# First stage of a four-layer graph network on one core: the order of x, the adjacency masks and the slice-logit fold

## Chip, core and metric

The kernel runs on one core of a Trainium2 chip. The metric is the device time of one execution in microseconds (us): the median of 3 runs was 2817.94 us (2809.52 to 2823.55). The execution that the profiler recorded took 2806.95 us, of which 2805.2 us lie between its first and its last instruction (the span).

## The reference, cut to what matters

The network has four layers on 2708 nodes with 256 features. Each layer adds a graph step over a dense 2708x2708 adjacency matrix (int32) and then a feed-forward step. The change touches the graph step of layer 0 and one small product of its feed-forward step:

```python
# graph step, features = layernorm(x)
Qn, Kn = cos_normalize(features @ Wq.T), cos_normalize(features @ Wk.T)   # 128 columns each
att = softmax(where(adj > 0, Kn @ Qn.T, NEG), axis=1)
prop = where(sum(adj, 1) > 0, att @ features, features)
x = x + 0.5 * prop + 0.5 * features
# feed-forward step, its slice weights
xm = (layernorm(x) @ W_x.T + b_x) per head                                # 8 heads of 64
sw = softmax((xm @ W_slice.T + b_slice) / max(temperature, 1e-6))
```

## The kernel before, in words

Nodes are cut into 22 tiles of 128 rows (NT = 22, the last has 20). The first stage, `cosine_gnn`, has two parts.

**Projection.** x (tile X, line 180) is read in three pieces and a rest: tiles 0 to 7 on SP's DMA queue, 8 to 15 on ACT's, 16 to 20 on SP's. `ln_stats` computes mean and variance of each tile on DVE (lines 144 and 145), their roots on ACT (147) and reciprocals on DVE (151). Then the 22 tiles go by 12 groups, ten pairs and two single tiles: `project` writes the normalised features F (DVE, line 108), transposes them on PE (tp, 225), copies them on ACT (ft, 227) and multiplies them by the weights wqk (pq, 123); `normalise` squares and sums on ACT (sq, 239), takes roots (nrm, 241 to 243), scales (qk, 245, DVE), transposes (pt, 251, PE) and copies to QK (254, half on DVE and half on ACT).

**Score blocks.** The 2708 target nodes are cut into 6 blocks, five of 512 columns and one of 148. For each block and each of the 22 tiles j: a score matmul into PSUM (273; three buffers named score), exp on ACT (275), multiplication by the mask on DVE (281), and up to four matmuls into the accumulators acc (284). In fp32 each of these matmuls stands as two instructions in the profile. After a block, DVE and ACT copy the accumulators and update X (293 to 301).

**Masks.** `columns(i0, iw)` fetches one block of the transposed adjacency in 8 pieces of up to 128x3x512 int32 (raw, 768 KB, line 194, SP's queue, four buffers) and turns each into bytes of the resident mask tile on DVE (198). Before, `columns` of the first two blocks stands ahead of the projection, and that of block n+2 at the head of block n. The whole rows of the adjacency (row, 1354 KB each, line 204, SP's queue, three buffers) are summed on ACT (`degree`, 210), one tile after every fourth exp.

**Fold.** `slice_logits` multiplies W_x by W_slice and the temperature ahead of everything, so that the slice step later needs one matrix wf and one bias bf (lines 326 to 363): 32 matmul instructions wfp (348), 16 bfp (357), 2 bfb (362), some small DVE work (343 to 360) and a copy on ACT (363). Its weights wx, bx, ws, bs and ti come over POOL's queue, and so does wqk. The mask tile occupies memory that the fold's tiles leave, so the memset of its last tile (165, POOL) and all conversions follow the fold.

**Order.** A scheduler in the tile framework puts each engine's instructions into one fixed order when the kernel is built; each engine then runs its list in that order. `issue_after(i)` makes the scheduler put what stands under it behind instruction i. SP's DMA queue is also a list in order: a request that waits for a free buffer holds all requests behind it. After the blocks, SP writes the mask to memory (kept, 303), and `clear_dispatch` writes 8 zero pieces of 2838 KB each (hs, 2235); before, the scheduler mixes these with the rows. The next stage, `slice_ffn`, runs over the 22 tiles with pl (wf), the slice softmax on DVE and ACT, and z; its weights outw, outb, wfx, hyin, hyout come over POOL's queue.

Of the kernel before, what the change touches and what calls it, by code (L numbers as in the profile page):

```python
# [8 lines left out]
F32 = mybir.dt.float32  # L9
# [3 lines left out]
ALU = mybir.AluOpType  # L13
# [3 lines left out]
P = 128  # L17
N = 2708
D = 256
# [16 lines left out]
def rows(t):  # L36
    return min(P, N - t * P)


def span(t):  # L40
    return slice(t * P, t * P + rows(t))


def chunks(width):

    return [(c, min(width, N - c)) for c in range(0, N, width)]
# [108 lines left out]
        return inverse_root(self.net, pool, self.mv[:, t0:t1, 1], 1.0, LN_EPS, "nr", self.rstd[:, t0:t1])  # L155


def cosine_gnn(net, ctx, kept, x_in):

# [4 lines left out]
    with ExitStack() as ctx:  # L166
        big = ctx.enter_context(tc.tile_pool(name="g0big", bufs=1))
        rawp = ctx.enter_context(tc.tile_pool(name="g0raw", bufs=4))
        rowp = ctx.enter_context(tc.tile_pool(name="g0row", bufs=3))
        F = big.tile([P, NT, D + 1], F32, name="F")  # L170
        QK = big.tile([P, 2, N], F32, name="QK")
        den = big.tile([P, NT], F32, name="den")
# [1 line left out]
        total = big.tile([P, NT], F32, name="total")  # L174

        nrm = big.tile([P, NT, 2], F32, name="nrm")
        w = net.load_weight(big, a["wqkT"], "wqk")
        full = N // P * P
        for t0, t1, engine in ((0, 8, nc.sync), (8, 16, nc.scalar), (16, NT - 1, nc.sync)):
            engine.dma_start(X[:, t0:t1, :], x_in[t0 * P : t1 * P].rearrange("(t p) d -> p t d", p=P))  # L180
        nc.scalar.dma_start(X[: N - full, NT - 1, :], x_in[full:])
        nc.gpsimd.memset(F[:, :, D : D + 1], 1.0)
# [3 lines left out]
        GR = 3  # L186
        groups = [range(t, min(t + GR, NT - 1)) for t in range(0, NT - 1, GR)] + [range(NT - 1, NT)]

        def columns(i0, iw):

            for g in groups:
                t0, n, r = g[0], len(g), rows(g[0])
                raw = rawp.tile([P, GR, 512], I32, name="raw")
                nc.sync.dma_start(
                    raw[:r, :n, :iw],
                    a["adjT"][t0 * P : t0 * P + (n - 1) * P + r, i0 : i0 + iw].rearrange("(t p) i -> p t i", p=r),
                )
                nc.vector.tensor_scalar(
                    net.mask[:r, t0 : t0 + n, i0 : i0 + iw], raw[:r, :n, :iw], 0.0, None, ALU.is_gt
                )  # L200

# [7 lines left out]
            r = rows(i)  # L209
            nc.scalar.activation(row[:r], row[:r], AF.Copy, accum_out=total[:r, i : i + 1])  # L210

        columns(*chunks(512)[0])
        columns(*chunks(512)[1])
        ln = net.ln_stats()
        with tc.tile_pool(name="g0p", bufs=2, space=PSUM) as psum, tc.tile_pool(name="g0w", bufs=3) as work:
            pairs = [range(t, t + 2) for t in range(0, NT - 2, 2)] + [range(NT - 2, NT - 1), range(NT - 1, NT)]
# [16 lines left out]
            def normalise(g):  # L233
                n, r, t0 = len(g), rows(g[0]), g[0]
                pq = held.pop(g)
                sq = work.tile([P, P], F32, name="sq")
                for k, t in enumerate(g):
                    for m in range(2):
                        nc.scalar.activation(sq[:r], pq[:r, k, m], AF.Square, accum_out=nrm[:r, t, m : m + 1])
                v = nrm[:r, t0 : t0 + n, :]  # L240
                nc.scalar.activation(v, v, AF.Sqrt)
                nc.vector.tensor_scalar(v, v, 1e-4, None, ALU.max)
                nc.vector.reciprocal(v, v)
                qk = work.tile([P, 2, 2, P], F32, name="qk")
                nc.vector.tensor_tensor(
                    qk[:r, :n], pq[:r, :n], v.unsqueeze(3).to_broadcast([r, n, 2, P]), ALU.mult
                )
                pt = psum.tile([P, 2, 2, P], F32, name="pt")
                for k in range(n):
                    for m in range(2):  # L250
                        nc.tensor.transpose(pt[:, m, k, :r], qk[:r, k, m], net.ident[:r, :r])
                nodes = slice(t0 * P, t0 * P + (n - 1) * P + r)
                for m, engine in ((0, nc.vector.tensor_copy), (1, nc.scalar.copy)):
                    engine(QK[:, m, nodes], pt[:, m].rearrange("p k b -> p (k b)")[:, : (n - 1) * P + r])

            for n, g in enumerate(pairs):
                project(g)
                if n:
                    normalise(pairs[n - 1])
            normalise(pairs[-1])  # L260
        work = ctx.enter_context(tc.tile_pool(name="g0work", bufs=3))
        psc = ctx.enter_context(tc.tile_pool(name="g0s", bufs=3, space=PSUM))
        pacc = ctx.enter_context(tc.tile_pool(name="g0a", bufs=1, space=PSUM))
        for n, (i0, iw) in enumerate(chunks(512)):
            its = tiles_of(i0, iw)
            adj_rows = {i: load_rows_of(i) for i in its}
            if n + 2 < len(chunks(512)):
                columns(*chunks(512)[n + 2])
            acc = [pacc.tile([P, D + 1], F32, name=f"acc{k}", tag=f"acc{k}") for k in range(len(its))]
            for j in range(NT):  # L270
                r = rows(j)
                ps = psc.tile([P, 512], F32, name="score")
                nc.tensor.matmul(ps[:r, :iw], QK[:, 0, span(j)], QK[:, 1, i0 : i0 + iw], start=True, stop=True)  # L273
                e = work.tile([P, 512], F32, name="e")
                exp = nc.scalar.activation(e[:r, :iw], ps[:r, :iw], AF.Exp)  # L275

                if j % 4 == 1 and 0 <= j // 4 - 1 < len(its):
                    i = its[j // 4 - 1]
                    with tc.issue_after(exp.ins):
                        degree(i, adj_rows[i])  # L280
                nc.vector.tensor_tensor(e[:r, :iw], e[:r, :iw], net.mask[:r, j, i0 : i0 + iw], ALU.mult)  # L281
                for k, i in enumerate(its):
                    ri = rows(i)
                    nc.tensor.matmul(  # L284
                        acc[k][:ri], e[:r, k * P : k * P + ri], F[:r, j, :], start=j == 0, stop=j == NT - 1
                    )
            nc.vector.tensor_scalar(
                deg[:, its[0] : its[-1] + 1], total[:, its[0] : its[-1] + 1], 0.0, None, ALU.is_gt
            )
# [10 lines left out]
                nc.vector.scalar_tensor_tensor(X[:r, i, :], g[:r, :D], s[:r, 0:1], X[:r, i, :], ALU.mult, ALU.add)  # L300
                nc.vector.scalar_tensor_tensor(X[:r, i, :], F[:r, i, :D], s[:r, 1:2], X[:r, i, :], ALU.mult, ALU.add)
        for t in range(NT):
            nc.sync.dma_start(kept[span(t), :], net.mask[: rows(t), t, :])
        nc.vector.tensor_scalar(net.empty, den, 0.0, None, ALU.is_equal)


def inverse_root(net, pool, v, scale, eps, name, out=None):
# [15 lines left out]
    return y if out is None else last  # L323


def slice_logits(net, pool):


    nc, tc, a = net.nc, net.tc, net.a
    H, G, HC = 8, 64, 512  # L330
    wf = pool.tile([P, 2, HC], F32, name="wf")
    bf = pool.tile([P, HC], F32, name="bf")
    with tc.tile_pool(name="s_f", bufs=1) as fp, tc.tile_pool(name="s_fp", bufs=1, space=PSUM) as psum:
        wx = fp.tile([64, H, D], F32, name="wx")
        nc.gpsimd.dma_start(wx, a["w_x"].rearrange("(h p) c -> p h c", p=64))
        bx = fp.tile([64, H], F32, name="bx")
        nc.gpsimd.dma_start(bx, a["b_xT"])
        ws = fp.tile([64, G], F32, name="ws")
        nc.gpsimd.dma_start(ws, a["w_sliceT"])
        bs = fp.tile([1, G], F32, name="bs")  # L340
        nc.gpsimd.dma_start(bs, a["b_slice"].partition_broadcast(1))
        ti = net.load_rows(fp, a["temperature"], H, "ti")
        nc.vector.tensor_scalar(ti, ti, 1e-6, None, ALU.max)
        nc.vector.reciprocal(ti, ti)
        for c in range(2):
            ps = psum.tile([P, H, G], F32, name=f"wfp{c}")
            for h in range(H):
                nc.tensor.matmul(ps[:, h, :], wx[:, h, c * P : (c + 1) * P], ws, start=True, stop=True)
            nc.vector.tensor_tensor(
                wf[:, c, :].rearrange("p (h g) -> p h g", g=G),  # L350
                ps,
                ti.unsqueeze(2).to_broadcast([P, H, G]),
                ALU.mult,
            )
        pb = psum.tile([1, H, G], F32, name="bfp")
        for h in range(H):
            nc.tensor.matmul(pb[:, h, :], bx[:, h : h + 1], ws, start=True, stop=True)
        b0 = fp.tile([1, H, G], F32, name="b0")
        nc.vector.tensor_tensor(b0, pb, bs.unsqueeze(1).to_broadcast([1, H, G]), ALU.add)
        nc.vector.tensor_tensor(b0, b0, ti[0:1].unsqueeze(2).to_broadcast([1, H, G]), ALU.mult)  # L360
        pbb = psum.tile([P, HC], F32, name="bfb")
        nc.tensor.matmul(pbb, net.ones[0:1, :], b0.rearrange("p h g -> p (h g)"), start=True, stop=True)
        nc.scalar.copy(bf, pbb)
    return wf, bf


def slice_ffn(net, wf, bf, early):
# [1839 lines left out]
def net_kernel(ctx, tc, a, out):  # L2207
# [4 lines left out]
    net.hs = dram.tile([Routing.E * CAP, D + 2], F32, name="hs")  # L2212
    with ExitStack() as graph:
        with ExitStack() as early:
            folded = slice_logits(net, early.enter_context(tc.tile_pool(name="s_wf", bufs=1, side="right")))
            cosine_gnn(net, graph, kept, a["x"])
            clear_dispatch(net, net.const)
            slice_ffn(net, *folded, early)
        with ExitStack() as mixture:
            biased_gnn(net, *top1_ffn(net, mixture))  # L2220
    with ExitStack() as mixture:
# [129 lines left out]
```

## Time and profile before

| what | value |
|---|---|
| median of 3 runs | 2817.94 us |
| profiled execution, span | 2806.95 us, 2805.2 us |
| busy share of the span: PE, DVE, ACT, POOL | 93%, 52%, 37%, 13% |
| mean granted TensorE clock | 0.965 |
| 0 to 77.5 us, up to the first score | PE busy 44.88 us, DVE 59.97 us |
| 77.5 to 407 us, the score blocks | PE busy 325.82 of 329.50 us |
| 407 us to the end, not touched by the diff but for its start | 2398.2 us |

The profile is read in views: busy time of each engine in stretches of the span, groups of instructions by line, who waited for whom, the chain of work that ended last (each step is followed back to what released it), and a timeline of single instructions. Times in these views count from the first instruction. A busy PE is one with matmuls in its pipe, not one at its peak rate.

### The profile page before, as it was taken

What the parts mean: (1) busy time and instruction counts of PE and PEld (TensorE: products, weight loads), DVE (VectorE), ACT (ScalarE), POOL (GpSimd) and SP (SyncE); (2) the same over time, 40 slices, a digit from 0 to 9 for tenths busy, and PEclk for the clock granted to TensorE, in tenths of its full rate; (3) what the DMA queues carried; (4) which work ended last, traced back from release to release, by engine and by line L of the source; (5) the groups of instructions that cost most, each with busy time, mean ns of one, the idle gap of its engine ahead of it and who ended that gap; (6) DMA issues with size and microseconds to landing.
All of it is one profiled execution on the core that took longest, in us unless ns stands there. A gap on an engine that the chain in (4) does not pass through costs nothing.

```text
span 2805.2 us, 32369 instructions
## 1 busy us (share of the span) xinstructions
PE 2603.2 (93%) x11710; PEld 1611.2 (57%) x11710; DVE 1454.0 (52%) x3102; ACT 1040.9 (37%) x1641; POOL 377.2 (13%) x470
## 2 busy tenths in 40 slices
PE   5999999798999999969799989999989999969998
PEld 4667746574333444558588743333346777757885
DVE  7753348543777776332554456554664222255555
ACT  3444443314565662321444322233332222234453
POOL 1000012100000001134130013323331111110002
PEclk9999999787999999989899999999999999989999
DMA  8899420000000002654310010000121111040001
GB/s 294 287 290 304 149 69 1 3 5 1 1 1 1 1 1 85 173 168 133 108 33 1 1 36 23 18 1 24 77 99 64 35 33 33 25 168 33 1 1 40
DMA packets 106874, 197.70 MB, mean 70 GB/s; under 512 B 8846, under 2 KB 63736, under 8 KB 103876
## 3 DMA queue, kind: packets, MB, share of 16 engines
q1 hardware_dynamic: 88010, 146.82, 16.9%
q0 software_dynamic: 14896, 43.89, 4.8%
q10 hardware_dynamic: 3806, 4.85, 0.6%
q8 instruction: 99, 1.62, 0.2%
q14 instruction: 63, 0.52, 0.1%
HBM read 135.82 MB, written 59.71 MB: 70 GB/s over the span
## 4 chain that ended last, share of the span: by engine, by line
PE 77%; DVE 8%; issue 5%; DMA 4%; ACT 3%; POOL 2%; SPq 0%; ACTq 0%; POOLq 0%; DVEq 0%
PE acc L1311 15%; PE acc L805 8%; PE acc L284 7%; PE h L2031 7%; PE den L816 4%; PE po L2063 4%; PE po L1872 4%; PE score L273 3%; PE sc L1852 3%; PE pv L123 3%; PE h L943 2%; PE sc L1818 2%; PE po L123 2%; DMA dys<-y,to 2%; PE pl L123 1%
## 5 line engine op out<-in xcount | busy, mean ns | idle before, releaser
L675 DVE SCALAR_TENSOR_TENSOR e<-e,mask 128x768 f32<-128x768 f32 (+2 forms) x264 | 412.1, 1576 | 304.4 <-ACT e L674 304.3
L674 ACT ACTIVATE e<-big_p,minus_one,ratio 128x768 f32<-128x768 f32 (+2 forms) x264 | 394.8, 1513 | 367.0 <-PE acc L1311 229.8
L1311 PE MATMUL acc<-V,e 128*128 128x257 f32 (+1 forms) x1936 | 433.5, 383 | 4.5 <-DVE e L675 4.4
L1311 PEld LDWEIGHTS acc<-V,e 128*128 128x128 f32 (+1 forms) x1936 | 352.3, 186 | 85.7 <-issue 32.1
L805 PE MATMUL acc<-e,V 128*64 128x512 f32 (+1 forms) x1056 | 242.7, 548 | 4.4 <-DVE e L675 4.4
L2031 PE MATMUL h<-w,ft 128*128 (+1 forms) x752 | 234.1, 453 | 0.5 <-DVE dso_far L1497 0.5
L284 PE MATMUL acc<-F,e 128*128 128x257 f32 x968 | 226.3, 384 | 3.0 <-DVE e L281 2.6
L284 PEld LDWEIGHTS acc<-F,e 128*128 128x128 f32 x968 | 173.4, 185 | 66.9 <-DVE e L281 28.4
L805 PEld LDWEIGHTS acc<-e,V 128*64 128x64 f32 x1056 | 107.9, 137 | 161.8 <-issue 129.2
L1852 PE MATMUL sc<-qt,kt 64*128 64x512 f32 (+5 forms) x568 | 170.1, 566 | 4.1 <-ACT e L1866 2.4
L2048 DVE TENSOR_TENSOR hh<-hh,h 128x682 f32<-128x682 f32 x47 | 40.7, 865 | 247.5 <-PE h L2031 247.5
L2031 PEld LDWEIGHTS h<-w,ft 128*128 128x128 f32 x752 | 135.9, 191 | 56.5 <-issue 1.8
L1866 ACT ACTIVATE e<-sc 128x1024 f32<-128x1024 f32 (+4 forms) x121 | 100.2, 857 | 183.1 <-PE sc L1852 167.8
L281 DVE TENSOR_TENSOR e<-e,mask 128x512 f32<-128x512 f32 (+2 forms) x132 | 80.4, 625 | 149.0 <-ACT e L275 147.3
L1878 DVE TENSOR_TENSOR sum<-sum,e 128x1024 f32<-128x1024 f32 (+5 forms) x95 | 104.7, 1102 | 74.5 <-ACT e L1866 71.2
L2063 PE MATMUL po<-w,ht 114*128 (+1 forms) x564 | 131.6, 383 | 5.3 <-DVE ht L2056 5.3
L275 ACT ACTIVATE e<-score 128x512 f32<-128x512 f32 (+2 forms) x132 | 69.7, 544 | 179.0 <-PE score L273 152.1
L1872 PE MATMUL po<-e,V 128*64 128x512 f32 (+4 forms) x484 | 112.3, 542 | 17.5 <-DVE e L1870 9.0
L816 PE MATMUL den<-e,low 128*3 128x512 f32 (+1 forms) x1056 | 123.8, 542 | 0.3 <-DVE e L675 0.3
L2063 PEld LDWEIGHTS po<-w,ht 114*128 114x128 f32 x564 | 107.5, 191 | 27.8 <-DVE ht L2056 12.9
L273 PE MATMUL score<-QK 128*128 128x512 f32 (+2 forms) x264 | 112.1, 554 | 1.2 <-ACT e L275 0.7
L1852 PEld LDWEIGHTS sc<-qt,kt 64*128 64x128 f32 (+1 forms) x568 | 58.4, 188 | 89.3 <-issue 74.0
(639 smaller groups left out, 3463.3 us busy)
## 6 DMA issues: line engine op xcount, KB each, us to landing
row<-in_adj SPq DMA_DIRECT2D x21, 1354.0 KB
raw<-in_adjT SPq DMA_DIRECT2D x35, 768.0 KB
hs<-zero SPq DMA_DIRECT2D x8, 2838.0 KB
hidden<-hr SPq DMA_DIRECT2D x32, 256.0 KB
wd<-in_f_wd SPq DMA_DIRECT2D x8, 1024.0 KB
kept<-mask SPq DMA_DIRECT2D x21, 338.5 KB
mask<-kept SPq DMA_DIRECT2D x21, 338.5 KB
w<-in_d_w1T SPq DMA_DIRECT2D x8, 682.0 KB
```

The costliest lines, as they stand in the source:

```text
L123: self.nc.tensor.matmul(out, lhsT[:, c, :], rhs[:, c, :], start=first and c == 0, stop=last and c == n - 1)
L273: nc.tensor.matmul(ps[:r, :iw], QK[:, 0, span(j)], QK[:, 1, i0 : i0 + iw], start=True, stop=True)
L284: nc.tensor.matmul(acc[k][:ri], e[:r, k * P : k * P + ri], F[:r, j, :], start=j == 0, stop=j == NT - 1)
L674: nc.scalar.activation(v, big_p[:, i], AF.Relu, bias=net.minus_one, scale=ratio)
L675: return nc.vector.scalar_tensor_tensor(v, v, 1.0, net.mask[:, j, i], ALU.add, ALU.mult)
L805: made = nc.tensor.matmul(acc[n][half, :iw], V[:, j, h, :], e[:, k, i0 : i0 + iw], start=j == 0, stop=j == NT - 1)
L816: made = nc.tensor.matmul(den[g : g + Q, :iw], low[:, j, h, Q - 1 - q : 2 * Q - 1 - q], e[:, k, i0 : i0 + iw], start=False, stop=j == NT - ...
L1311: nc.tensor.matmul(acc[k][:ri], e[:, k * P : k * P + ri], V[:, j, :], start=j == 0, stop=j == NT - 1)
L1852: nc.tensor.matmul(by_pairs(ps[:r, g])[:, :, o:], kt[b, span(j)], qt[b, :, o:iw], start=True, stop=True)
L1872: nc.tensor.matmul(by_pairs(po[b])[:, :, o:], V[:r, j, g, :], by_pairs(e[:r, g])[:, :, o:], start=j == 0, stop=j == last,)
L2031: last = nc.tensor.matmul(halves[s, n][:, q, :HALF], fts[s][:, c, :], weights.w13[n][:, es[s], c, q * HALF : (q + 1) * HALF], start=c == 0 ...
L2063: last = nc.tensor.matmul(po, ht[:KP, k, :], w2[:KP, es[s], k, :], start=k == 0, stop=k == KC - 1)
```

## The change

- x comes in four pieces and a rest; wx moves from POOL's queue to SP's, behind x; wqk from POOL's queue to the head of ACT's.
- `columns` becomes a generator. The conversions of block 0 (`own`) are put one behind the normalisation of each of two late pairs, and then one behind the masked product of every third tile of block 0. Those of block n+1 (`ahead`) are put behind the masked product of tiles 1, 4, 7, ... 19 and 21 of block n.
- The rows have two buffers, not three. `degree` stands behind the exps of tiles 9, 12, 15 and 18. The rows of block 0 are asked for at its tile 9 behind the pieces asked for by then.
- The fold's matmuls stand between the score blocks, one step behind each of blocks 1 to 4, and take a score buffer in PSUM; its weights stay in the stage's pool.
- `clear_dispatch` is put behind the last kept store.

```diff
-        w = net.load_weight(big, a["wqkT"], "wqk")
+        w = net.load_weight(big, a["wqkT"], "wqk", nc.scalar)
-        for t0, t1, engine in ((0, 8, nc.sync), (8, 16, nc.scalar), (16, NT - 1, nc.sync)):
+        for t0, t1, engine in ((0, 4, nc.sync), (4, 8, nc.sync), (8, 16, nc.scalar), (16, NT - 1, nc.sync)):
...
-        rowp = ctx.enter_context(tc.tile_pool(name="g0row", bufs=3))
+        rowp = ctx.enter_context(tc.tile_pool(name="g0row", bufs=2))
...
-                nc.vector.tensor_scalar(
+                yield nc.vector.tensor_scalar(
                     net.mask[:r, t0 : t0 + n, i0 : i0 + iw], raw[:r, :n, :iw], 0.0, None, ALU.is_gt
                 )
...
-        columns(*chunks(512)[0])
-        columns(*chunks(512)[1])
+        own = columns(*chunks(512)[0])
+        folded.load(big)
...
                 if n:
-                    normalise(pairs[n - 1])
+                    done = normalise(pairs[n - 1])
+                    if len(pairs) - n in (2, 4):
+                        with tc.issue_after(done.ins):
+                            next(own)
...
+        fold = folded.fold(psc, "score")
         for n, (i0, iw) in enumerate(chunks(512)):
             its = tiles_of(i0, iw)
-            adj_rows = {i: load_rows_of(i) for i in its}
-            if n + 2 < len(chunks(512)):
-                columns(*chunks(512)[n + 2])
+            ahead = columns(*chunks(512)[n + 1]) if n + 1 < len(chunks(512)) else iter(())
+            if n:
+                adj_rows = {i: load_rows_of(i) for i in its}
...
-                if j % 4 == 1 and 0 <= j // 4 - 1 < len(its):
-                    i = its[j // 4 - 1]
+                if n == 0 and j == 9:
+                    with tc.issue_after(raws[-1].ins):
+                        adj_rows = {i: load_rows_of(i) for i in its}
+                if j % 3 == 0 and 0 <= j // 3 - 3 < len(its):
+                    i = its[j // 3 - 3]
                     with tc.issue_after(exp.ins):
                         degree(i, adj_rows[i])
-                nc.vector.tensor_tensor(e[:r, :iw], e[:r, :iw], net.mask[:r, j, i0 : i0 + iw], ALU.mult)
+                masked = nc.vector.tensor_tensor(e[:r, :iw], e[:r, :iw], net.mask[:r, j, i0 : i0 + iw], ALU.mult)
+                with tc.issue_after(masked.ins):
+                    if j % GR == 0 and n == 0:
+                        next(own, None)
+                    if j % GR == 1 or j == NT - 1:
+                        next(ahead, None)
...
+            if 0 < n < 5:
+                with tc.issue_after(last.ins):
+                    next(fold)
...
-            folded = slice_logits(net, early.enter_context(tc.tile_pool(name="s_wf", bufs=1, side="right")))
-            cosine_gnn(net, graph, kept, a["x"])
-            clear_dispatch(net, net.const)
-            slice_ffn(net, *folded, early)
+            folded = SliceLogits(net, early.enter_context(tc.tile_pool(name="s_wf", bufs=1, side="right")))
+            stored = cosine_gnn(net, graph, kept, a["x"], folded)
+            with tc.issue_after(stored.ins):
+                clear_dispatch(net, net.const)
+            slice_ffn(net, folded.wf, folded.bf, early)
```

The new `SliceLogits.fold` holds the old statements in four steps: the bias product bfp with its two DVE operations; bfb with the copy bf; the first half of wf; the second half. Each step takes one buffer of the score pool.

## Prediction

> **What bounds the kernel now.** I read four views. First the chain of work that ended last, cut to the first 560 us: before the first score it is not PE's work.
>
> ```profile
> 0.82 11.73 DMA X<-in_x
> ...
> 27.31 2.08 PE bfb L362 x2
> 29.42 6.73 DVE mask L198 x4
> 36.15 1.62 DVE F L108 x5
> ...
> 77.49 6.25 PE score L273 x10
> ```
>
> See the order: x (12.55 us), the fold's end (29.4), mask conversions, and the first score only at 77.49. Second, the waits of the first 130 us and the groups of instructions there:
>
> ```profile
> POOL mask L165 <- PE bfb L362: 23.6, 1, 23.6
> L198 DVE TENSOR_SCALAR mask<-raw 128x1536 uint8<-128x1536 int32 (+1 forms) x34 | 53.1, 1587 | 6.9 <-DMA raw<-in_adjT 6.0 <-PE bfb L362 0.9
> L348 PE MATMUL wfp<-ws,wx 64*128 64x64 f32 x32 | 7.1, 419 | 12.5 <-DMA ws<-in_w_sliceT 12.5
> L357 PE MATMUL bfp<-ws,bx 64*1 64x64 f32 x16 | 1.9, 308 | 0.0
> L362 PE MATMUL bfb<-b,ones 1*128 1x512 f32 x2 | 2.1, 1136 | 6.0 <-DVE b L360 6.0
> ```
>
> The mask's memory is held by the fold for 23.6 us, and 53.1 us of conversions follow on DVE. Third, busy time by stretch (us, then busy us of PE, PEld, DVE, ACT, POOL, granted clock, DMA share, GB/s):
>
> ```profile
> 30.10:77.50 47.40, 33.96 (x177) 26.46 (x177) 42.91 (x76) 26.47 (x125) 1.70 (x1) 1.00 0.79 265
> 77.50:140.90 63.40, 62.16 (x225) 42.32 (x226) 45.44 (x54) 25.15 (x35) 0.00 (x0) 0.97 0.85 298
> 140.90:201.00 60.10, 58.67 (x222) 40.96 (x222) 30.55 (x78) 26.19 (x36) 0.00 (x0) 1.00 0.98 286
> 201.00:259.40 58.40, 58.34 (x222) 40.97 (x221) 22.14 (x63) 25.91 (x36) 0.00 (x0) 1.00 1.07 309
> ```
>
> During the projection DVE is busy 42.91 of 47.40 us: it is the bound. In block 2, without conversions, PE is busy 58.34 of 58.40 us: it is the bound, and what stands on PE there costs its full length. Blocks 0 and 1, which share DVE with conversions, lose only 1.2 and 1.4 us of PE. Fourth, the timeline shows how close a group of three tiles runs in a block:
>
> ```profile
> 105.64 2.74 PE L273 MATMUL score<-QK 128*128 128x512 f32 x6
> 107.33 0.69 DVE L281 TENSOR_TENSOR e<-e,mask 128x512 f32<-128x512 f32 x1 [0.85 <-ACT e L275]
> 108.22 5.37 PE L284 MATMUL acc<-F,e 128*128 128x257 f32 x24
> ```
>
> With the scores from S, the first masked product ends at S+2.38 and its accumulation starts at S+2.58: no slack.
>
> **The change part by part.** I read the order in which the changed kernel's instructions stand on each engine, and put durations of the rows on it.
>
> *1. x and the fold ahead of the projection.* DVE's list has eleven tile statistics (tiles 0 to 10) before the first F, so the piece X[8:16] gates it. Ahead of its end on ACT's queue stand wqk and itself, 1.31 MB; with as much sent for SP that is 2.6 MB. Before, 2.50 MB had moved by 11.25 us (222 GB/s); 0.77 MB by 5 us (154 GB/s) and then the 334 GB/s of 5 to 7.5 us would give 2.6 MB at 10.5 us. I take 11. Tile 8's statistic stood at 16.08, so DVE's list moves up by 5.1 us, and the fold's operations leave it (2.7 us by starts): the last F of the first twelve ends at 28.55 - 7.8 = 20.8 us. PE no longer waits for bfb: its first transposes can run at 14 instead of 30.15. Roots on ACT (the fifth at 17.5), four squares at 0.40 and two ft copies at 0.47, then nrm and qk put the first pt near 23.0, against 39.21.
>
> [...]
>
> *2. Projection without conversions.* From the first pt to the last were 37.5 us for 11 groups, 3.41 each, with a 1.66 us conversion between most. Without: pt to the DVE half of QK 0.69, 0.46 to the ACT half, 0.27 for it, and nrm through qk to the next pt 1.49 (57.15 to 58.64), 2.9 us. PE's own work is 2.8, ACT's 2.55. Eight such, 23.2; the short last groups as before less a conversion, 2.4 + 1.5 + 1.6 + 0.75 = 6.3; the two conversions left, half hidden, 1.7. First score: 23.0 + 23.2 + 6.3 + 1.7 = 54.2 us, so **-23.3 us**. Bounds: 3.41 kept, 61.3 us, -16; ACT alone the limit, about 50, -27.
>
> *3. Conversions beside the scores.* Six conversions of block 0 itself and, in each block, 8 of the next one move under PE's bound. Where the list has product, conversion, product inside a group of three, the second product starts at S+3.96 and its accumulation at S+4.85, while PE is done with the first at S+4.31: 0.5 us. So stand six groups of block 0 (3.0, where 1.3 was idle before: +1.7) and three groups of blocks 1, 2 and 3 (+4.5); block 4 converts narrow pieces within the slack. Bounds: nothing, as blocks 0 and 1 lost little; or the whole 1.66 in all 15 groups, 25 us. I take 0.5, worked from the group's own starts. At the block ends PE's list now has five scores (4.3 us) while DVE finishes X in 3.6: the 1.4 us stall behind block 0 goes, -1.4.
>
> *4. DMA.* A raw buffer is asked for when its conversion four places earlier is done: 16 us ahead in block 0, 31 us later. Block 0 needs 14 MB, 220 GB/s over 63 us, blocks 1 to 3 190; 298 and 309 were moved. Rows with two buffers are asked for 6 tiles, 16 us, ahead, and a waiting row holds the raws behind it. I cost this at nothing; the cover is the 16 us against 10.1 us, the longest landing in the chain (104.62). hs, 22.7 MB, moves behind kept, by my estimate (300 GB/s) 350 to 430 us, beside POOL's weights; outb then lands a few us later, while PE has three tiles of f in hand; hs is not used before 1731 us. Nothing.
>
> *5. degree on the last exp of a group.* Before, two groups a block ran 5.47 instead of 5.20 us. -0.5 x 5 = -2.5 us; bounds 0 and -2.7.
>
> *6. Fold on PE.* It leaves a stretch that part 1 has counted and comes onto the bound: 32 wfp at 0.13 (a warm pt's pitch; 0.22 as they ran at 12.49), 16 bfp at 0.06 to 0.12, bfb 2 x 0.43 (1.04 as it ran): 4.2 + 1.4 + 0.9 = **+6.5**, bounds 5.6 and 11. Its DVE work (0.67 each) still fits under five scores.
>
> *7. Start of the slice stage.* Its list now has the first tile's softmax before the second tile's tp and pl, so three pl (1.73 each) follow instead of filling. The softmax itself ends 2.3 us sooner without its neighbour's operations; the second pt comes near 17.6 instead of 16.0 us after the first tp: +1.6, bounds 0 and 4.
>
> **Sum:** -23.3 + 1.7 + 4.5 - 1.4 - 2.5 + 6.5 + 1.6 = **-12.9 us**. Against the profiled execution, 2806.95 - 12.9 = 2794 us (span about 2792). The median of the runs shown is 11 us above that execution, so I put the same difference on it: 2817.94 - 12.9 = 2805 us.
>
> **Rivals.**
> A. *The blocks cover everything.* Blocks 0 and 1 speak for it: conversions there cost PE almost nothing. Then conversions cost 0 and the idle 1.3 goes, the fold is 5.6, the slice start 0: -23.3 - 1.3 - 1.4 - 2.5 + 5.6 = -22.9, 2795 us. Against it: those conversions were placed freely, these are pinned.
> B. *The start gains little.* ACT (26.47 us busy of 47.40) and the pq-to-pt loop keep 3.41 us a group, and x lands at 12.5 as before: first score 24.5 + 37.5 + 0.75 = 62.8, -14.7 + 10.4 = -4, 2814 us. For it: several qk waited for ACT, not for a conversion. Against: DVE was 90% busy.
> C. *Slower: the row takes the place.* degree is in ACT's list, exps stand behind it, and with two buffers a row is asked for only 16 us ahead. If it lands d later than that, all 20 rows of the wide blocks cost PE d: from d = 1.35 us (20 x 1.35 = 27, against the -13) the kernel is slower by over 0.5%; at d = 2, 2845 us. For it: row requests ran up to 11.5 us on SP, and raws stand in the same queue. Against: the rate needed is two thirds of what was moved.
>
> **How the numbers follow.** Forecast 0.64, A 0.18, B 0.11, C 0.07. A measurement of this kernel can tell about 0.5%, 14 us, from no change, and the forecast lies almost on that bound: faster 0.27 of its 0.64 and A's 0.17, 0.44; same 0.48; slower 0.08. The range goes from the low bounds together (-27 + 3 = -24, and a few us of the runs' spread) to the high bound of the start with the fold's (-16 + 17 = +1, and the spread): 2790 to 2822 us.
>
> **What would show it.** Right: the first score at 50 to 58 us; X[8:16], not X[0:4], before the first F; PE over 97% busy in blocks 1 to 4 with waits of about 0.5 us for DVE's masked product at tiles 14, 17 and 20; each block 59 to 62 us; ACT never waiting for a row. Wrong: DVE waiting for raw by more than a few us in blocks (DMA), a first score after 60 (B), wfp at 0.22 us in the blocks, or any shift of work behind 520 us.

## The result and the profile after

The changed kernel takes 2818.65 us (median of 20 runs, 2804.42 to 2828.73), the kernel before beside it 2818.02 us (20 runs). The ratio is 1.0005, with a 95% interval from 0.9994 to 1.0016: **no difference**. The forecast of 2805 us did not come.

The profiled execution of the changed kernel took 2817.16 us, that of before 2806.95, but the latter lies 11 us under its own median. So I compare places in the program and not whole spans. "u" below is the first transpose of u (hp<-ident,u), the first product behind the slice stage's sums; from there on both kernels issue the same instructions.

| place (us) | before | after | after minus before |
|---|---|---|---|
| first score | 77.49 | 58.47 | -19.0 |
| end of the last accumulation of the blocks | 407.11 | 403.70 | -3.4 |
| first tp of the slice stage | 410.95 | 407.48 | -3.5 |
| last sw (the start of the last tile's sw<-pl,bf) | 508.14 | 509.32 | +1.2 |
| u | 525.75 | 529.90 | +4.2 |
| first accumulation into acc<-V,e | 1399.70 | 1403.09 | +3.4 |

The start gave 19.0 us. The six blocks took back 345.23 - 329.62 = 15.6, the slice stage 101.84 - 97.19 = 4.7 (first tp to last sw), and the way from the last sw to u 20.58 - 17.61 = 3.0. That is all of it: -19.0 + 15.6 - 0.1 + 4.7 + 3.0 = +4.2 us. Later stages, in which the same instructions stand in the same order, add what differs from execution to execution; the medians differ by 0.6.

First the chain of work that ended last. Where before had x, the fold, conversions and the first score at 77.49, it now has two lines:

```profile
1.33 13.25 DMA X<-in_x
58.47 5.40 PE score L284 x8
```

X still ends its transfer only at 14.6 us. In the waits of the first 410 us (in total, times, longest) that piece is the longest wait for X, and the masked products cost TensorE 3.8 us altogether:

```profile
DVE bnst L144 <- DMA X<-in_x: 9.7, 3, 4.9
...
PE acc L304 <- DVE e L296: 3.8, 14, 0.5
```

Of the 14 waits eleven, those of blocks 0 to 2 in the middle of a group, last 0.22 to 0.26 us. No wait for a raw or a row stands in that list. The groups say the same of the conversions (idle before them 0.0) and give the fold's own cost:

```profile
L201 DVE TENSOR_SCALAR mask<-raw 128x1536 uint8<-128x1536 int32 (+3 forms) x48 | 66.5, 1386 | 0.0
...
L397 PE MATMUL fold<-ws,wx 64*128 64x64 f32 x32 | 4.5, 297 | 0.0
...
L386 PE MATMUL fold<-ws,bx 64*1 64x64 f32 x16 | 1.1, 216 | 0.0
```

Now blocks 2, 3 and 4 by stretch (us, busy us of PE, PEld, DVE, ACT, POOL, granted clock, DMA share, GB/s). Before, blocks 2 to 4 took 58.3 to 58.4 us, all at a clock of 1.00:

```profile
179.60:242.00 62.40, 61.66 (x238) 42.12 (x237) 34.91 (x73) 26.27 (x36) 0.00 (x0) 0.97 0.53 178
242.00:302.50 60.50, 60.00 (x225) 41.29 (x224) 34.55 (x74) 26.91 (x37) 0.00 (x0) 1.00 0.48 160
302.50:367.10 64.60, 64.10 (x238) 43.95 (x237) 26.13 (x72) 26.03 (x36) 0.00 (x0) 0.95 0.59 198
```

TensorE is busy for over 98% of each, as forecast, but the blocks are up to 6 us longer: its clock is not always 1.00. The microseconds around the first wfp run, behind block 3, show where it falls:

```profile
303.00:304.00 1.00, 1.00 (x10) 1.00 (x10) 1.00 (x5) 0.38 (x1) 0.00 (x0) 1.00 0.00 0
304.00:305.00 1.00, 1.00 (x8) 1.00 (x7) 0.07 (x1) 0.00 (x0) 0.00 (x0) 0.68 0.00 0
305.00:306.00 1.00, 1.00 (x3) 0.57 (x3) 0.70 (x3) 0.00 (x0) 0.00 (x0) 0.50 0.00 0
...
311.00:312.00 1.00, 1.00 (x4) 0.47 (x3) 1.00 (x3) 0.31 (x1) 0.00 (x0) 0.91 0.00 0
```

TensorE is never idle here, yet from 304.4 to 311.2 it gets half its clock (0.68 is 0.36 us at full and 0.64 us at half). The same happens behind bfp (181.5 to 184.9) and behind the second wfp (369.2 to 372.6). Half of 6.8 + 3.4 + 3.4 us, up to **6.8 us**, is a cost that no term of the prediction had. What it does to the eight scores that open a block stands in the timeline of the chain: 6.59 us behind the first wfp (305.26), 3.63 us behind bfb (243.60), where the clock stayed.

### The profile page after: what moved, and what is told of

It is laid out like the page before. It is cut to its first block, busy times and chain, and to the rows that moved or that the text cites. A ratio compares the mean times of both kernels' runs of the same rounds, so it can differ in the third digit from the quotient of the medians.

```text
span 2815.4 us, 32374 instructions
## 1 busy us (share of the span) xinstructions
PE 2619.8 (93%) x11710; PEld 1616.1 (57%) x11710; DVE 1454.9 (52%) x3102; ACT 1042.4 (37%) x1641; POOL 374.8 (13%) x468
## 4 chain that ended last, share of the span: by engine, by line
PE 79%; DVE 7%; issue 4%; ACT 4%; DMA 4%; POOL 2%; ACTq 0%; POOLq 0%; DVEq 0%; SPq 0%
PE acc L1351 15%; PE acc L845 8%; PE acc L304 7%; PE h L2071 7%; PE den L856 4%; PE po L2103 4%; PE po L1912 4%; PE sc L1892 3%; PE score L284 3%; PE pv L123 3%; PE h L983 2%; PE sc L1858 2%; PE po L123 2%; DMA dys<-y,to 2%; PE pl L123 1%
```

## Experiments

Theory 1: the fold's small matmuls cost their own 6.6 us and pull the clock down behind them. Theory 2: the slice stage's loss is one of order on its engines. Theory 3: the start is short because X[8:16] lands late. The rivals are named with each run. Times of medians are compared with the kernel before on the same chip; where an effect is smaller than these can tell, I compare the places of the table above.

**No fold.** All fold operations left out, wf and bf filled with a constant.

```
-            if 0 < n < 5:
-                with tc.issue_after(last.ins):
-                    next(fold)
+        nc.gpsimd.memset(self.wf, 0.01)
+        nc.gpsimd.memset(self.bf, 0.01)
```

> The changed kernel without any of the fold's operations (wf and bf are filled with a constant instead, so the slice logits are not the reference's); everything else stays. Theory 1 (the fold's 64-column matmuls cost their own 6.2 us on TensorE and, behind each run of them, half the granted clock for 3 to 6.5 us more): the six score blocks, 345.6 us from the first score in the changed kernel, shrink by 12 to 13 us to about 333, and no stretch in blocks 1 to 5 shows a granted clock of 0.5. Rival (the clock falls there for another reason, or the conversions pinned between the products cost the rest): only the 6 us of the matmuls go, the blocks stay at about 339, and the clock still falls at 181, 305 or 370 us. The first score stays at 58.5 us under both, and the slice stage keeps its late second tile, since only the fold goes. Time: 2806 under the theory, 2812 under the rival.

The blocks took 333.5 us (345.23 with the fold), from the first score at 58.19 us to the end of the last accumulation:

```profile
389.27 2.40 PE L303 MATMUL acc<-F,e 128*128 128x257 f32 x8 [0.37 <-DVE e L295]
```

The clock stayed at 1.00 behind block 0's first microseconds, and the time was 0.9972 of the kernel before (0.9955 to 0.9988). So the fold costs the blocks 345.2 - 333.5 = 11.7 us. The kernel with X[8:16] in two pieces (below) splits this: it has the same fold, no fall of the clock behind it, and blocks of 339.96 us. By these three executions 6.5 us are the fold's own length and 5.3 the clock's, somewhat under the 6.8 of the sum above. The rest of the change in the blocks, conversions, degree and block ends together, costs 333.5 - 329.6 = 3.9 us. The slice stage kept its loss (102.5 us), as both expected.

**Fold spread out.** One head behind each tile's accumulations, in a PSUM bank of its own.

```
+                if 0 < n < 5 and 2 <= j < 14:
+                    with tc.issue_after(last.ins):
+                        next(fold, None)
```

> The changed kernel with the same fold, its matmuls handed out one head behind each tile's accumulation inside blocks 1 to 4 (in a PSUM bank of its own) instead of in one run between blocks. Theory 1 (a run of 64-column matmuls makes the clock fall): the matmuls still cost about 6 us, but the clock stays at 1.00 in blocks 1 to 5, and the blocks take 338 to 340 us instead of 345.6. Rival (the fold's matmuls cost their own length and nothing else, and the falls of the clock have another cause): 345 us again, with falls of the clock at the block ends. Time: 2812 under theory 1, 2818 under the rival.

No clock below 1.00 was left in any block, as theory 1 had it: without a run of small matmuls it did not fall. (One execution is not proof: with X[8:16] in two pieces, below, it did not fall behind the runs either. The count over all profiles, further down, carries more.) But the blocks took 343.33 us, hardly less than 345.23, and the time was 1.0017 (1.0002 to 1.0033). The timeline shows why the theory's 338 to 340 was wrong:

```profile
194.47 0.43 PE L399 MATMUL fold<-ws,wx 64*128 64x64 f32 x2
194.83 2.00 PE L305 MATMUL acc<-F,e 128*128 128x257 f32 x8
196.76 0.43 PE L399 MATMUL fold<-ws,wx 64*128 64x64 f32 x2
```

A tile's accumulations with one head between them come every 2.29 us (196.76 - 194.47), without one every 1.73 (16 of them, two tiles, take 3.47 in the chain). A head alone thus costs 0.56 us, in a run 0.29 (2.3 / 8). Sixteen such, eight bfp heads at 0.40 and bfb at 1.1 are 13.3 us. The blocks grew by 343.3 - 333.5 = 9.8 us, and here the clock had not fallen at the first score, which costs the kernel without a fold 1.4 (block 0 took 62.07 us there and 60.63 here), so by 11.2. That is 2 us under my estimate, and nearly the 11.7 of the fold in runs: the same sum, paid another way.

**Weights of the slice stage later.** The four loads behind the fifth tile's logits.

```
-            wfx = net.load_weight(wp, a["w_fxT"], "wfx")
...
+                    if t == 5:
+                        wfx = net.load_weight(wp, a["w_fxT"], "wfx")
```

> The changed kernel with the four weight loads of the slice stage (wfx, bfx, hyin, hyout) asked for by GpSimd's queue behind the fifth tile's logits, not ahead of the first memset of f. Theory 2 (those four loads, which now wait for the end of the last block because the fold's weights take the memory, stand 2.7 us ahead of f on GpSimd, and the second tile's transposes fall behind the first tile's softmax): the second tp comes about 4 us after the first pl instead of 10, and from the first tp to the last sw the stage takes 97 us instead of 101.8, as before the change. Rival (hs's 22.7 MB of zeros, which move until 460 us in the changed kernel and were through before the stage in the kernel before, cost the stage its 4.7 us): 101 to 102 us again. Time: 2813 under theory 2, 2818 under the rival.

First tp to last sw took 96.72 us (101.84 in the changed kernel, 97.19 before), u came at 522.66, and the time was 0.9976 (0.9957 to 0.9995). hs's zeros still moved beside it, at 295 GB/s, so they are not the reason. GpSimd in the changed kernel has loads between outb and the memset of f that used to run at 390 us, inside the last block; first the kernel before, then two lines of the changed kernel:

```profile
390.06 0.72 POOL L93 DMA_DIRECT2D wfx<-in_w_fxT  x1 [358.25 <-DVE deg L287]
...
408.64 0.71 POOL L93 DMA_DIRECT2D wfx<-in_w_fxT  x1
...
411.38 0.19 POOL L438 MEMSET f<- 128x1 f32 x3
```

and TensorE's list puts the second tile's tp behind the first tile's softmax; first the changed kernel, then this one:

```profile
408.66 3.78 PE L123 MATMUL pl<-wf,ft 128*128 128x512 f32 x4 [0.52 <-ACT ft L442]
417.11 1.09 PE L465 MATMUL pt<-ident,sw 128*128 128x128 f32 x4 [4.67 <-DVE sw L458]
...
418.85 0.64 PE L116 MATMUL tp<-ident,f 128*128 128x128 f32 x2
```

```profile
409.39 3.52 PE L123 MATMUL pl<-wf,ft 128*128 128x512 f32 x4 [0.52 <-ACT ft L437]
412.74 0.38 PE L116 MATMUL tp<-ident,f 128*128 128x128 f32 x2
413.59 1.99 PE L123 MATMUL pl<-wf,ft 128*128 128x512 f32 x4 [0.46 <-ACT ft L437]
```

The gap of 10 us between the first tile's logits and the second tile's transposes is gone. The two kernels with unread matmuls (below) agree: in them the four loads come as late, from 406.7 and 406.3 us, but the memset of f stands ahead of them, at 387 us, and the stage takes 97.1 and 95.8 us. So it is their place ahead of f that costs, not the late loads by themselves. That the loads moved because the pools lie otherwise in SBUF (the fold's weights now live in the first stage's pool) is argued from the code and not tried by itself.

**X[8:16] on SyncE's queue.**

```
-((8, 16, nc.scalar), (16, NT - 1, nc.sync))
+((8, 16, nc.sync), (16, NT - 1, nc.scalar))
```

> The changed kernel with X[8:16] asked for on SyncE's queue ahead of wx and the raws, and X[16:21] on ScalarE's in its place. Theory 3 (X[8:16] on ScalarE's queue shares the DMA engines with the raws asked for on SyncE's, so it lands only at 14.67 us when 3.8 MB have moved, and it gates the first F): X[8:16] lands at 9.5 to 11 us, the first F comes 3.5 to 5 us sooner, and the first score at 54 to 55.5 us instead of 58.47. Rival (the list of statistics ahead of the first F and ScalarE's work set the start): the first score moves by less than 1.5 us. Time: 2814 to 2815 under theory 3, 2818 under the rival.

In between: tile 8's statistic started at 13.23 us (14.67), the first score at 55.98 (-2.5). The first tp came 5.6 us sooner, at 10.93, but ScalarE's third root stands ahead of its first ft copy and needs X[8:16] too. Ratio 0.9992 (0.9972 to 1.0012).

**Fold in the projection**, and **all three cures so far together**. In both the fold's steps stand behind the transposes of the fourth, sixth, eighth and ninth pair.

```
+                    if n in (4, 6, 8, 9):
+                        with tc.issue_after(turned.ins):
+                            next(fold)
```

> The changed kernel with nothing moved but the fold, from between the score blocks into the projection, where TensorE is idle for 8 of the last 14 us. Theory 1: the blocks take 332 us, as without a fold, with no granted clock of 0.5 in them after the first 62 us; the projection grows by 1 to 3 us, since the runs of 64-column matmuls (2.3 us each) only partly fit into its waits; sum -10 to -12 us. Rival (the fold costs the projection what it cost the blocks, 12.6 us): first score near 71 us, sum near 0.

> The changed kernel with the fold moved into the projection (bfp, bfb, wfp, wfp behind the transposes of the fourth, sixth, eighth and ninth pair, in two PSUM banks of its own), X[8:16] on SyncE's queue, and the slice stage's four weight loads behind the fifth tile's logits. By the parts measured so far: first score 56 us plus 1 to 3 for the fold; blocks 332 us instead of 345.2; first tp to last sw 96.7 us instead of 101.8; last sw to the transposes of u 17.7 us instead of 20.6. Sum against the changed kernel: -2.5 + 2 - 13 - 5 - 3 = -21 us, against the kernel before -17 us (ratio 0.994). Rival (what is taken away at one place is waited for at the next, as in the kernel whose fold was spread out): less than 8 us better than the changed kernel, ratio to before 0.998 or more.

The blocks fell to 333.5 us in both, with full clock from 70.3 us to their end. But the first score came at 64.89 in the one (+6.4) and 66.63 in the other (10.7 later than with X on SyncE's queue alone): I had expected 1 to 3. I read it so, without a test of its own: TensorE's waits there are parts of one chain between engines, and a run put into it delays what follows. The clock also fell there, from 52.1 to 55.5 us in the first and from 49.8 to 63.4 in the second. Ratios 0.9994 (0.9977 to 1.0011) and 0.9942 (0.9921 to 0.9964).

**What kind of run makes the clock fall.** Unread matmuls in place of the fold, of another kind behind each block.

```
+            if n < 5 and PLAN[n]:
+                count, k, m, cols = PLAN[n]
+                spare = psc.tile([P, 512], F32, name="spare", tag="score")
```

> The changed kernel without the fold, and in its place matmuls into a spare PSUM tile whose result nobody reads (the slice logits' weights are constants, so they are not the reference's). Behind block 0: 16 instructions of 64 columns with the array full (128 rows by 128); behind block 1: 16 of 64 columns with 64 rows by 128, as the fold's wfp; behind block 2: 6 of 512 columns, array full; behind block 3: 8 of 64 columns, 64 rows by 128; behind block 4 nothing. Theory 1 (short columns make the clock fall): falls to 0.5 behind blocks 0 and 1, none behind 2 and 4, and behind 3 perhaps none, since 1 us of them is half a run. Rival A (the half-filled array makes it fall): none behind block 0, one behind 1. Rival B (chance of the time since the last fall): no pattern, also behind 2 or 4.

> As the run above, with the places changed. Behind block 0: 6 instructions of 512 columns, array full; behind block 1: 16 of 64 columns, array full; behind block 2: 8 of 256 columns, array full; behind block 3: 16 of 128 columns, array full; behind block 4: 4 of 64 columns, 64 rows by 128. Theory 1: a fall behind block 1 alone, perhaps behind 3 (128 columns are between). Rival A (half-filled array): behind block 4 alone. Rival B (chance or place): behind block 0 again, as in the changed kernel.

Behind block 0 of the first run stand 16 of 64 columns with all 128 rows, behind block 1 the same with 64 rows. Both take 2.0 us:

```profile
121.00:123.00 2.00, 2.00 (x18) 2.00 (x18) 2.00 (x12) 0.38 (x1) 0.00 (x0) 1.00 0.86 307
123.00:125.00 2.00, 2.00 (x6) 0.81 (x5) 1.37 (x7) 0.83 (x2) 0.00 (x0) 1.00 0.06 23
...
185.00:187.00 2.00, 2.00 (x6) 0.92 (x5) 1.20 (x9) 0.42 (x1) 0.00 (x0) 0.73 0.04 16
187.00:189.00 2.00, 2.00 (x4) 0.77 (x3) 1.25 (x4) 0.77 (x2) 0.00 (x0) 0.50 0.00 0
```

Only behind the second did the clock fall (185.9 to 189.3). It did not behind 512, 256 or 128 columns, or 4 or 8 instructions with 64 rows (one execution of each kernel). So theory 1's "short columns" was wrong in this point and Rival A right: in these two executions the fall went with the rows and not with the columns. The two runs also read other tiles (F and wqk with all rows, ws and wx with 64); the next kernel has ws and wx with all rows.

**Two heads to a matmul.** w_slice twice on the diagonal of a 128x128 tile, 128 rows of w_x against it.

```
-            nc.tensor.matmul(ps[:, h, :], self.wx[:, h, c * P : (c + 1) * P], self.ws, ...)
+            two = ps[:, 2 * h : 2 * h + 2, :].rearrange("p h g -> p (h g)")
+            nc.tensor.matmul(two, self.wx[:, h, c * P : (c + 1) * P], self.ws, ...)
```

> The changed kernel with the same fold at the same places, but two heads to a matmul: 128 rows of w_x against a 128x128 tile that holds w_slice twice on its diagonal (128 columns, 8 instructions instead of 16 a run). Theory 1 as the runs of unread matmuls left it (a run of 2 us with half the array's rows makes the clock fall, a run of 64 or 128 columns with all rows does not): wfp takes about 1.1 us a run instead of 2.3, no granted clock of 0.5 behind blocks 2, 3 and 4; bfp, with one output row, is open, it was 0.5 to 1 us and may still pull the clock down; blocks 335.5 to 337.5 us instead of 345.2, time 2809. Rival (any break in the stream of scores and accumulations of over 1 us makes it fall): falls behind the same blocks as before, 340 us or more.

The blocks took 338.34 us, the time was 0.9973 (0.9957 to 0.9989). A wfp run is half as long, and the scores behind it run at full speed:

```profile
361.74 1.16 PE L402 MATMUL fold<-ws,wx 128*128 128x128 f32 x8
362.73 2.22 PE L284 MATMUL score<-QK 128*128 128x148 f32 x12
```

Twelve such scores took 3.37 us in the changed kernel. The clock fell once, behind bfb (240.6 to 244.0), where it had not fallen in the changed kernel. So one and the same run was followed by a fall in some executions and not in others. Over all profiles: wfp-like runs of 16 instructions with 64 rows between blocks 8 of 11, bfp with 64 rows 3 of 5, bfb with one row 2 of 8; bfp with 128 rows by one column 0 of 3; runs that fill the array, 128 rows by 128, **0 of 12** (six of 2.0 to 2.9 us, as long as wfp, and six of 1.2).

**Raws held back.** The first four raws wait for a copy that needs tile 15's statistics.

```
+                if i0 == 0 and g[0] < 4 * GR:
+                    nc.vector.tensor_copy(raw[:1, 0, :1], ln[0][:1, 15:16])
```

> The changed kernel with the first four raw pieces held back: each waits for a one-element copy that needs the statistics of tile 15, so X lands with only wqk, ws and wx beside it. Theory 3 (the raws took the bandwidth that X[8:16] waited for): X[8:16] lands at 10 to 11 us instead of 14.67, as the prediction had it, the first F at 11 to 12.5, and the first score at 54 to 55 us instead of 58.47; no conversion waits for a raw later. Rival (ScalarE's queue itself is slow with X[8:16], or the statistics' list sets the start): it lands after 13 us, or the first score stays above 57.

The rival was right. On VectorE, tile 8's statistic still waited until 14.01 us:

```profile
14.01 0.43 DVE L144 BATCH_NORM_STATS2 bnst<-X 128x6 f32<-128x256 f32 x1 [4.22 <-DMA X<-in_x]
```

The first score came at 57.99. The raws are not what X waits for, but for 0.7 us of it. Places up to u are those of the changed kernel (529.64), though its ratio is 0.9974 (0.9957 to 0.9992) against 1.0005: these 0.3% have no place in the stages up to u of this execution, which at 2815.66 us was 6 us over the kernel's median. Where they come from stays open.

**X[8:16] in two pieces, ahead of wqk.** All engines keep their lists.

```
+((8, 12, nc.scalar), (4, 8, nc.sync), (12, 16, nc.scalar), (16, NT - 1, nc.sync))
```

> The changed kernel with X[8:16] in two pieces, X[8:12] and X[12:16], first on ScalarE's queue, and wqk behind them; nothing else changes, the lists of all engines stay the same. Theory 3a (the piece is late because ScalarE's queue gets less than half of what moves, 1.3 of 3.5 MB by 14 us, and one semaphore covers all of it): X[8:12] lands at 7.5 to 9.5 us, the first F comes at 9 to 11 us instead of 15.95, X[12:16] lands by 13, and the first score at 53 to 55 us instead of 58.47; wqk, now last, lands at about 14 and holds the first pq to that. Rival 3b (behind the first F another thing is as late: the later pieces of X, wqk, or ScalarE's list): X[8:12] lands early but the first score stays above 57.

X[8:12] no longer held anything, but now X[4:8] did (wait until 9.83 us instead of 7.93). First F at 12.92 (15.95), first score at 56.21: 2.3 us, less than theory 3a's 3.5 to 5.5, and more than Rival 3b's 1.5: the next piece is late instead. The order changed how the queues share. SyncE's packets (q1) and ScalarE's (q10) from 2 to 6 us, with their MB, in the changed kernel and then here:

```profile
q1 hardware_dynamic: 878, 0.88, 68.5%
q10 hardware_dynamic: 310, 0.30, 22.3%
...
q1 hardware_dynamic: 635, 0.63, 52.2%
q10 hardware_dynamic: 527, 0.53, 37.8%
```

In all twelve profiles with wqk at the head of its queue ScalarE's moves 281 to 310 packets there; with X ahead of wqk it moves 527 here and 516 in the last kernel below. This kernel has the changed kernel's fold as it is, and in this execution the clock did not fall once behind it: blocks 339.96 us. Ratio 0.9999 (0.9982 to 1.0016).

**The cures together**: two heads to a matmul and the later weights, with the raws held back in the first and X in two pieces in the second.

> The three cures together: raws held back until X has landed, the fold with two heads to a matmul, the slice stage's weight loads behind the fifth tile's logits. Expected from the parts, against the changed kernel: start -4, blocks -9, slice stage -5, sum -18 us (ratio to the kernel before 0.994), the transposes of u at 511 to 514 us instead of 529.9. Rival (the parts wait for each other): less than 10 us, u after 520.

> The cures of the run named best, with X[8:16] in two pieces ahead of wqk in place of the raws held back. If theory 3a holds: first score 53 to 55, transposes of u at 508 to 512 us, ratio to the kernel before 0.993 to 0.995. Under rival 3b it does what best did: first score 57, u at 513, 0.9956.

2801.57 us, ratio 0.9956 (0.9941 to 0.9971), u at 513.61; and 2803.13 us, 0.9964 (0.9948 to 0.9980), u at 516.82. Both are some 0.4% faster than the kernel before, and their intervals lie under the changed kernel's (0.9994 to 1.0016). With the version that has the fold in the projection (0.9942) their intervals overlap; which of the three is best stays open.

## Why the prediction was wrong, step by step

- **1 and 2, the start: -23.3 forecast, -19.0 measured.** The step that failed is "I take 11" for the landing of X[8:16]. It landed at 14.67, 3.7 us later, and the first pt came 3.7 us later than forecast (26.74 for 23.0); from there to the first score it was 31.7 us for 31.2. So the chain behind the landing was right, the estimate of the transfer wrong. That X[8:16] is the piece that gates was right. What failed is "with as much sent for SP", which no run shows for the whole of the transfer. The sum of both was near: 2.54 MB moved from 2 to 10 us, where I wanted 2.6 by 10.5. But ScalarE's queue had 0.98 MB of it and not 1.31, since from 2 to 6 us it moved 310 packets and SyncE's 878. That lag came with wqk at its head, which the change itself put there (the run with X ahead of wqk also splits the piece). The rest of the piece then met a lower rate: after 10 us all queues together moved 181 to 251 GB/s, not 334, at a share of the DMA engines of 0.85 to 1.16. (The kernel before had shown 221 to 245 GB/s from 7 to 11 us.) With the raws held back the packets were the same, 871 and 310; the rate was 273 and 321 GB/s from 10 to 12 us, then 221 and 176. Why the rate falls stays open.
- Even shares came only later: SyncE's queue and ScalarE's moved 356 and 355 packets from 6 to 8 us, 306 and 308 from 8 to 10.
- **3 and 5, conversions, block ends, degree: +2.3 together, 3.9 measured** (no fold against before). A conversion in a group did cost 0.5 us. It shows as a wait of only 0.23, but such groups follow each other at 8.27 us (75.34, 83.61, 91.88 in the changed kernel), those without one at 7.78 (333.54, 341.32, 349.10 without a fold). There were 14 such groups without a fold and eleven with it, not 15. Most of the miss is in block 0: +2.7 us (62.07 for 59.34), where +1.7 - 0.5 was forecast. The parts beside the conversions were not measured alone.
- **4, DMA: nothing, right.** No conversion and no degree waited for a transfer in the blocks. hs's 22.7 MB beside the slice stage cost nothing that the later-weights run could show.
- **6, the fold: +6.5 forecast, 11.7 measured.** Its own length was right (6.5). The term missed that the scores behind it run at half the clock (5.3). I had taken all matmuls behind it at the durations of a full clock; before the change the fold stood ahead of the projection, where no score followed it. Its low bound, 5.6, is not the sum of its parts (4.2 + 1.0 + 0.9 = 6.1), and the low bounds of parts 3 to 7 add up to +1.5 (0 - 1.4 - 2.7 + 5.6 + 0), not +3; the forecast does not hang on them.
- **7, the slice stage: +1.6 forecast (0 to 4), 4.7 measured.** I read the new order of its list, and the first pt did come sooner (9.6 us after the first tp, 12.1 before). But the second pt came 21.1 us after the first tp, not 17.6. I had not seen that the order's cause, four loads on GpSimd, was itself an effect of the change, and I took the matmuls there at full clock: pt, z and tp from 417.1 to 420.4 us ran at half (pt 1.09 us, 0.65 before; granted 0.50 from 412 to 420 us, 0.71 before).
- **Behind 520 us: nothing forecast, +3.0 by u.** The small matmuls there ran at half the clock for longer (granted 0.66 from last sw to u, 0.81 before). From last sw to u the kernels above, which change nothing there, took 17.7 to 20.6 us, so I take this to be mostly the clock's chance; no run tests it.

By measured terms: -19.0 + 3.9 + 11.7 + 4.7 + 3.0 = +4.3 us, against +4.2 read at u.

Of the rivals, A was wrong in both of its points: by it conversions, block ends and degree give back 5.2 us and the fold costs 5.6, where +3.9 and 11.7 were measured. B's late x came, its groups of 3.41 us did not (the first seven took 2.9 each, as forecast). C's wait for a row did not come.

## What to carry to other kernels

Small work that is moved onto the bound engine is to be costed with what it does to that engine's clock and to its neighbours: a fold whose runs fill half the array's rows or fewer cost nearly twice its length here (11.7 us for 6.5), and behind wfp packed to full rows (1.16 us a run) the clock did not fall. Where an edit moves buffers from one pool to another, look at which later loads now wait for other memory, and what stands behind them on their queue. A gain at the start is worth what the last piece allows, so the landing time of that one piece deserves bounds from the share that its own queue gets and from a rate seen at full queues, not from the best stretch.

## What the hardware showed that I had not expected

TensorE's clock fell to half while its records show it busy for every microsecond, 0.6 to 2.7 us after a run of matmuls with 64 rows, or with a single row or column, began, and it stayed there for 3.4 or 6.8 us. In the profiles of the kernel before and of the changed one all changes of the clock lie whole multiples of 3.413 us apart, to 1 ns; in nine of the other kernels, by the mean clock of each microsecond from 56 to 545 us, to 0.01 us.

Divide the score blocks at that spacing, and weight the time of each matmul (from its start to the next) with the share of the 128 rows that it fills. This is an estimate of mine from the start and the rows of each matmul in the traces. Of the pieces at full clock that lie wholly in the blocks of the changed kernel, three come under 0.40, and behind each of them the clock fell: 0.38 (178.1 to 181.5 us), 0.31 (300.9 to 304.4) and 0.33 (365.8 to 369.2). The second holds most of the last tile's accumulations, which fill 20 rows and end every block, and then wfp. The piece with bfb has 0.45, all others 0.65 or more, and no fall followed. In the kernel before, without a fold there, no piece comes under 0.52, and none ended in a fall. With X[8:16] in two pieces the division meets the same runs elsewhere, no piece came under 0.46, and the clock did not fall. But behind the unread run with 64 rows it did, and the piece ahead of that fall (182.5 to 185.9 us) has 0.54. So the estimate goes with most of these falls and not with all; what brings them about no run shows.

The mean granted clock of an execution also goes with most of its time. Over the 20 runs of the changed kernel it lies between 0.954 and 0.962, and the time falls by 2.6 us for each 0.001 of it (correlation -0.88); over 31 runs of the kernel before, 2.5 us (-0.85), over the 9 of the first version with the cures together 2.4 (-0.99). The mean is 0.957 for the changed kernel and 0.960 for the kernel before in those runs, which were made at another time. On the fitted lines at 0.960 the two stand at 2812 and 2815 us. That is no hidden gain of 3 us, because the falls behind the fold belong to the change: in its profiled execution, 13.6 us at half the clock are 0.0024 of the mean, most of the 0.003 between the two. The spread of some 20 us between executions goes with the clock.
